# Table windows with their three parts stacked down the partitions, and a softmax table joined per block of nodes

## The chip, the cores and the metric

One core of a Trainium2 chip runs the whole kernel in one launch. The metric is the device time of one execution in microseconds. The engines are TensorE (PE, with its weight loads PEld), VectorE (DVE), ScalarE (ACT), GpSimd (POOL) and SyncE (SP). DMAs are issued from SP, ACT and, for the indirect ones, POOL.

## The reference

A graph of N = 6250 nodes with F = 128 features and E = 100000 edges. Edges come sorted by their destination `dst`; the sources `src` are random. `x` goes through two layers, each added to its input and normalised:

```python
# layer 0: attention over the edges, 8 heads of 16
q, k, v = (x @ W.T + b).reshape(N, 8, 16)           # for Wq, Wk, Wv
scores = sum(q[src] * k[dst], -1) / 4 + edge_attr_8
ex = exp(scores - segment_max(scores, src)[src])
weights = ex / segment_sum(ex, src)[src]             # softmax over a source's edges
out = segment_sum(v[src] * weights, dst) @ Wo.T + bo
x = layernorm(x + out)
# layer 1: a message of each edge, summed at its source
h = silu(concat(x[src], x[dst], edge_attr_2) @ eW1 + eb1)
fe = silu(h @ eW2 + eb2)
agg = segment_sum(fe, src)
x = layernorm(x + silu(concat(x, agg) @ nW1 + nb1) @ nW2 + nb2)
```

All of it is float32.

## The kernel before, in words

The edges are padded to 784 tiles of 128, taken in 49 chunks of 16 tiles (`UC`). The first 9 chunks are the near region (destinations in the first two blocks of 128 nodes), the other 40 the far region. `REG` holds the two; `r` is 0 for near and 1 for far. A node block is 128 rows; there are 49.

**How a row of a table reaches an edge.** A table such as q is held in DRAM as three bfloat16 parts side by side, whose sum is the float32 value. Edges of a sorted run touch few nodes that lie near each other, so a *window* of 128 consecutive rows is loaded, 128 partitions of 3 x 128 values. A one-hot matrix with a column for each edge (`hot_of`, an `is_equal` of a broadcast row of offsets with the partition's number) picks each edge's row on PE, one product for each of the three parts, summed in PSUM. `regs` reads a window's first row from an index tile into a register for the DMA.

**Stages, in order.**

1. *Sort*, beside the projections to q, k, v. The edges come by `dst` and leave by `src`. A chunk's loads (`prep_loads`: L734 `lob`, L736 `drow`, L740 `sk`, L742 `ri`, L745 four windows `kw`, one per four tiles) go out on SP. `chain` (L765 to 780) walks the 16 tiles: ACT copies a running count (`cs`, L777), PE adds a tile's histogram to it (`base`, L778) and looks up each edge's place (`look`, L780). `spread_k` (L787) fetches k's rows with `ohd` (L758) and ACT copies them into the record `stg` (L789). `rank` (L762) is a DVE count. `pick` and `send` (L794 to 809) work out the positions, and 16 scatters on POOL (L126) write records of 141 floats to `xs`. Near-region scores run in between once their records are there; `near_scores` writes the near region's softmax statistics per node to the DRAM table `near_tab`.
2. *Scores and messages* of the far region, 40 chunks. The steps are laid out as a plan: each step of a chunk has a lag in chunks, the list is sorted by time and emitted in that order, with a few rules (`held`, `run`) on what must come first. `fetch` loads the sorted records and the q windows (L518), `turn` transposes the index columns and writes the edge features' rows for later, `score` is the q products (L587) times k (L590, L591), `soft` and `stat` form maximum and sum of each source inside the chunk and add them into `stat_r` (L657, L663). `merge` joins a window of `stat_r` with one of `near_tab`: it loads `z` (L942) and the v windows `vw` (L945), copies the window of `stat_r` (L949, `tmp`), transposes it (L954), reduces (L955), pools the parts (`pooled`), takes the reciprocal and splits the result in three (`lw`); 48 products (L968) look it up and DVE and ACT form the weight `wt`. `message` multiplies v's rows (L979) with it (L982) and POOL scatters 16 tiles to `xmsg` (L126), back in the order of `dst`. The near region's messages run in the same plan and are summed by one-hot products (L1016 to 1021).
3. *Sum by destination* (L1099 to 1112) and the *node stage* (L1124 to 1165): the residual, the norm, and two tables for the edge layer, `a` for sources (three parts) and `b` for destinations (float32).
4. *Edge MLP*, in steps of four tiles, 160 far and 36 near. `loads_of` makes the one-hots (L1184, L1188), loads the edge features' 18 rows (`eft`, L1200) and the windows of a (`aw`, L1204). `pre_of` gathers b's rows on POOL (L118, `bt`), transposes them into PSUM (L1217; near steps use products with `b_near`, L1222), adds the edge features' product (L1224, `wef`) and a's three (L1228). `second` is the second layer (L1237, L1240) and `total` sums by source (L1251 `ohf`, L1255, L1259). The node MLP of a group of blocks follows as soon as its blocks are complete (L1265 on).

Windows are taken every two tiles in the near region and every four in the far one (`WT = (2, 4)`).

Of the kernel before, what the change touches and what calls it, by code (L numbers as in the profile page):

```python
# [32 lines left out]
WT = (2, 4)  # L33
PER_BLOCK = (377.5, 1671.0)
SLACK = (512.0, 1024.0)
# [17 lines left out]
def tile_gnn(  # L53
# [28 lines left out]
    q3_tab, k3_tab, v3_tab, a3_tab = (dram.tile([NW, 3 * F], BF16, name=f"{n}3_tab") for n in "qkva")  # L82
    b_tab = dram.tile([NP, F], F32, name="b_tab")
    ka_tab = dram.tile([NW, 3 * F], BF16, name="ka_tab")
    near_tab = dram.tile([NW, 16], F32, name="near_tab")
# [52 lines left out]

    def rows_of(table, j0, n):
        return table[j0 * P:(j0 + n) * P, :].rearrange("(j p) f -> p j f", p=P)  # L140
# [11 lines left out]
    for b in range(1, AB):  # L152
# [3 lines left out]
        nc.vector.tensor_scalar_add(iota_f2[b], iota_f, float(b * P))  # L156
    cnt = const.tile([P, NB], F32, name="cnt")
    xflag = const.tile([1, 1], I32, name="xflag")
    dq = const.tile([P, TU], F32, name="dq")
    d0q = const.tile([1, 208], I32, name="d0q")  # L160
    slo = const.tile([P, TU], F32, name="slo")
    s0i = [const.tile([1, n], I32, name=f"s0i{i}") for i, n in enumerate((80, 176))]
# [18 lines left out]
    def load_keys(r):  # L181
# [13 lines left out]
        for i in range(g):  # L195
            nc.sync.dma_start(d0r[r][:, i:i + 1],
                              bass.AP(tensor=dst_r.tensor, offset=dst_r.offset + (t0 + i * p) * P,
                                      ap=[[4 * P, p // 4], [0, 4], [1, 1]]))
# [70 lines left out]
    def rows_of_keys(r):  # L269
# [8 lines left out]
        if r == 0:  # L278
            nc.gpsimd.memset(none, -1.0)
            zero = ks.tile([P, 3 * F], BF16, name="zero")  # L280
            nc.gpsimd.memset(zero, 0.0)
            for tab in (k3_tab, q3_tab, v3_tab, a3_tab):
                nc.sync.dma_start(tab[NP:NW, :], zero)
# [17 lines left out]
        if r == 0:  # L301
            nc.vector.tensor_scalar_min(d0q[:, :nt // 4], kd[r][0:1, 0:nt:4], float(AB * P - 1))
        else:
            nc.vector.tensor_copy(d0q[:, t0 // 4:(t0 + nt) // 4], kd[r][0:1, 0:nt:4])
# [8 lines left out]
        if r == 0:  # L313
            nc.vector.memset(bad, 0.0)
            nc.vector.memset(d0q[:, NQ:], 0)
        b = bad[:, 4 * r:4 * r + 4]
        over = ks.tile([p, g, P], F32, name=f"over{r}")
# [4 lines left out]
        nc.vector.tensor_single_scalar(b[:p, 1:2], b[:p, 1:2], float(P), ALU.is_ge)  # L322
# [3 lines left out]
        if r == 1:  # L326
            d0qf = ks.tile([1, nt // 4], F32, name="d0qf")
            nc.vector.tensor_copy(d0qf, d0q[:, t0 // 4:NQ])
# [4 lines left out]
                                 spread[:, :, None].to_broadcast([P, nt // 4, 4]))  # L333
            yield
# [46 lines left out]
    def counts_fit():  # L381
# [6 lines left out]
        half = kp.tile([P, 2], F32, name="half")  # L388
        nc.vector.tensor_single_scalar(half[:, 1:2], iota_p, float(P // 2), ALU.is_ge)
        nc.vector.tensor_scalar(half[:, 0:1], half[:, 1:2], -1.0, 1.0, ALU.mult, ALU.add)  # L390
        sums = bank()[:, :NB]
        nc.tensor.matmul(sums[:2, :], half, cnts[1], start=True, stop=True)
        nc.vector.tensor_reduce(b[:2, 2:3], sums[:2, :], AX.X, ALU.min)
        nc.vector.tensor_single_scalar(b[:2, 2:3], b[:2, 2:3], float(4 * P), ALU.is_lt)
# [17 lines left out]
    def project_qv():  # L412
# [8 lines left out]
        nc.scalar.mul(bqv[:, 0], bqv[:, 0], D ** -0.5)  # L421
        for j0 in range(0, NB, 2):
# [12 lines left out]
            for a in range(3):  # L435
# [5 lines left out]
                for i, tab in enumerate((q3_tab, v3_tab)):  # L441
                    nc.sync.dma_start(
                        tab[j0 * P:(j0 + n) * P, a * F:(a + 1) * F].rearrange("(j p) f -> p j f", p=P),
# [5 lines left out]
    def weights():  # L449
# [21 lines left out]
        nc.sync.dma_start(parts.rearrange("i r f -> r i f"), p3)  # L471
        for i in range(3):
            for f in range(2):
                nc.sync.dma_start(wef[6 * i + 3 * f:6 * i + 3 * f + 3, :], parts[i, f:f + 1, :].to_broadcast([3, F]))
# [4 lines left out]

    def scorer(r, sp, bank_q, bank_x, deep, dsti=None):  # L480

        c0, n = REG[r]
        nw = UC // WT[r]
        works = {}
        s0b = sp.tile([P, n * nw], F32, name="s0b", bufs=1)
        minus = sp.tile([P, 1], F32, name="minus", bufs=1)
        equal = [sp.tile([P, P + 1], BF16, name=f"equal{i}", bufs=1) for i in range(3)]
        v96 = [sp.tile([P, UC, 96], BF16, name=f"v96_{i}", bufs=1) for i in range(2)]
        diag8 = sp.tile([P, UC], BF16, name="diag8", bufs=1)

        def begin():
# [3 lines left out]
                                           ap=[[XW, 1], [WT[r] * P * XW, n * nw], [1, 1]]))  # L495
# [6 lines left out]
            nc.vector.memset(s0i[r][:, n * nw:], 0)  # L502
# [1478 lines left out]
```

## Time and profile before

| | us |
|---|---|
| median of 3 runs | 4228.26 (4224.49 to 4229.2) |
| profiled execution | 4211.11 |
| its span | 4209.2 |

| engine | busy us | share of the span |
|---|---|---|
| PE (matmul) | 2643.5 | 63% |
| PEld (weight load) | 2030.1 | 48% |
| POOL | 2156.6 | 51% |
| DVE | 1994.6 | 47% |
| ACT | 861.8 | 20% |

The mean granted TensorE clock was 0.713. In a profile, a group's row gives the line of the kernel, the engine, the operation with output and inputs by the program's names, and how often it ran; then the busy time and the mean of one in ns; then how long the engine had been idle just before, and what ended most of that. "issue" means that nothing in the profile held it. A matmul's duration is from its issue to its end, and matmuls overlap; a matmul group's mean is therefore longer than what one more product costs.

### The profile page before, as it was taken

The numbers are of one execution on the slowest core, as the hardware profiler recorded it, in microseconds if no ns is written. First come the engines' busy times: TensorE is split into PE (matmuls) and PEld (weight loads), VectorE is DVE, ScalarE is ACT, GpSimd is POOL, SyncE is SP. The second block draws the span as 40 slices with busy tenths as digits, with TensorE's granted clock in tenths as the row PEclk, the third lists the DMA queues.
The fourth block names the chain that finished last, engine by engine and source line by source line (L and its number), as shares of the span: only waits on it lengthen the run. The fifth ranks groups of instructions, "written<-read, shape, count | busy, mean of one in ns | idle before, by whom it ended". The sixth has DMA issues, their size and how long they took to land. (4 is left out here: it accounts for less than half of the span.)

```text
span 4209.2 us, 65902 instructions
## 1 busy us (share of the span) xinstructions
PE 2643.5 (63%) x22552; PEld 2030.1 (48%) x22552; DVE 1994.6 (47%) x6056; ACT 861.8 (20%) x2688; POOL 2156.6 (51%) x2119
## 2 busy tenths in 40 slices
PE   6546674444444225555655666565895999898988
PEld 4444443333333224444544555454883666665655
DVE  6655335454545525555555556554892222222232
ACT  2222232122222111111111111110022222222222
POOL 3455544555555551445445444556216666666663
PEclk8555555566555556666676777576897899999999
DMA  5433545444543315434434344431754333333341
GB/s 180 130 118 103 143 138 168 139 151 132 167 130 100 110 60 142 135 109 133 122 113 127 114 120 117 138 98 50 281 197 128 109 100 98 99 110 98 101 124 46
DMA packets 492378, 523.75 MB, mean 124 GB/s; under 512 B 155562, under 2 KB 417117, under 8 KB 486912
## 3 DMA queue, kind: packets, MB, share of 16 engines
q1 hardware_dynamic: 399150, 345.09, 28.3%
q0 software_dynamic: 66048, 140.62, 10.9%
q10 hardware_dynamic: 26834, 33.73, 2.5%
q8 instruction: 180, 2.95, 0.3%
q14 instruction: 166, 1.36, 0.1%
HBM read 391.11 MB, written 128.06 MB: 123 GB/s over the span
## 5 line engine op out<-in xcount | busy, mean ns | idle before, releaser
L126 POOL DMA_INDIRECT xs<-stg,posi x784 | 803.9, 1025 | 766.1 <-ACT cs L777 337.0
L126 POOL DMA_INDIRECT xmsg<-msg,at x640 | 648.7, 1014 | 722.1 <-issue 409.4
L118 POOL DMA_INDIRECT bt<-b_tab,dsti x640 | 640.5, 1001 | 333.4 <-issue 165.4
L778 PE MATMUL base<-hi,lo 128*128 128x49 bf16 x784 | 169.6, 216 | 547.3 <-ACT cs L777 333.5
L780 PEld LDWEIGHTS <-hit 128*128 128x128 bf16 x2352 | 145.7, 116 | 546.5 <-issue 531.0
L1259 DVE TENSOR_TENSOR stat_r<-stat_r,ps 128x128 f32 x232 | 66.3, 286 | 645.7 <-PE ps L1255 223.4
L787 PE MATMUL kx<-kw,ohd 128*128 128x128 bf16 x2352 | 265.5, 284 | 97.0 <-issue 56.9
L762 DVE TENSOR_SCALAR_CACHE_REDUCE junk<-sk,meta 128x127 bf16<-128x127 int16 x784 | 298.1, 435 | 11.4 <-DMA sk<-skew 4.8
L777 ACT CAST cs<-base 128x49 bf16<-128x49 f32 x784 | 160.7, 205 | 638.3 <-remote 286.4
L787 PEld LDWEIGHTS <-ohd 128*128 128x128 bf16 x2352 | 213.9, 131 | 136.1 <-issue 129.3
L587 PEld LDWEIGHTS <-oht 128*128 128x128 bf16 x2352 | 219.3, 134 | 124.3 <-issue 63.8
L1255 PE MATMUL ps<-ohf,fe 128*128 128x128 f32 x1568 | 231.4, 292 | 52.1 <-issue 28.5
L587 PE MATMUL qv<-qw,oht 128*128 128x128 bf16 x1920 | 200.5, 287 | 97.7 <-DVE oht L576 36.3
L1240 PE MATMUL po<-w_sb,ht 128*128 128x128 f32 x1568 | 245.6, 301 | 18.7 <-issue 9.4
L1255 PEld LDWEIGHTS ps<-ohf,fe 128*128 128x128 f32 x1568 | 208.8, 205 | 62.0 <-issue 33.9
L1240 PEld LDWEIGHTS po<-w_sb,ht 128*128 128x128 f32 x1568 | 205.2, 203 | 66.8 <-issue 49.4
L979 PE MATMUL qv<-vw,oht 128*128 128x128 bf16 x1920 | 188.5, 257 | 74.2 <-DVE pr L590 34.0
L1232 ACT ACTIVATE ht<-pre 128x512 f32<-128x512 f32 x196 | 116.9, 597 | 493.1 <-PE pre L1228 199.6
L979 PEld LDWEIGHTS <-oht 128*128 128x128 bf16 x1920 | 152.9, 117 | 122.6 <-issue 92.3
L223 DVE TENSOR_TENSOR lo<-iota_e,lo_c 128x2048 bf16<-128x2048 bf16 x98 | 119.0, 1215 | 150.6 <-remote 80.2
L780 PE MATMUL look<-st_b,hit 128*128 128x49 bf16 x1568 | 164.3, 211 | 27.1 <-DVE sel L794 17.0
L1228 PE MATMUL pre<-oht,aw 128*128 128x512 bf16 (+1 forms) x696 | 171.9, 365 | 12.8 <-issue 12.4
(303 smaller groups left out, 5228.8 us busy)
## 6 DMA issues: line engine op xcount, KB each, us to landing
st<-xs SPq DMA_DIRECT2D x49, 1128.0 KB
srow<-slo_row SPq DMA_DIRECT2D x98, 512.0 KB
lob<-lob_row SPq DMA_DIRECT2D x49, 512.0 KB
drow<-dlo_row SPq DMA_DIRECT2D x49, 512.0 KB
sk<-skew SPq DMA_DIRECT2D x49, 508.0 KB
qw<-q_tab SPq DMA_DIRECT2D x232, 96.0 KB
vw<-v_tab SPq DMA_DIRECT2D x232, 96.0 KB
aw<-a_tab SPq DMA_DIRECT2D x232, 96.0 KB
```

Source lines behind the costliest of these rows:

```text
L118: nc.gpsimd.indirect_dma_start(out=dst, out_offset=None, in_=table, in_offset=bass.IndirectOffsetOnAxis(ap=idx, axis=0))
L126: apart(nc.gpsimd.indirect_dma_start(out=table, out_offset=bass.IndirectOffsetOnAxis(ap=idx, axis=0), in_=src, in_offset=None), group)
L587: nc.tensor.matmul(qe[:, i, :], w["oh"][:, 4 * q + i, :], w["qw"][:, (4 * q + i) // WT[r], k, :], start=(k == 0), stop=(k == 2))
L762: nc.vector.tensor_scalar(junk, w["sk"][:, :, j], meta[:, c * UC + j, 0:1], 0.0, ALU.is_equal, ALU.add, accum_out=w["rank"][:, j:j + 1])
L777: nc.scalar.copy(cs, base)
L778: nc.tensor.matmul(base, lo, hi, start=False, stop=False, skip_group_check=True)
L780: nc.tensor.matmul(w["look"][:, j - 8 * h, :], w["hit"][:, j, :], tab, start=(i == 0), stop=(i == 2))
L787: nc.tensor.matmul(kx[:, i, :], w["ohd"][:, 4 * q + i, :], w["kw"][:, q, a, :], start=(a == 0), stop=(a == 2))
L979: nc.tensor.matmul(ve[:, i, :], w["oh"][:, 4 * q + i, :], w["vw"][:, (4 * q + i) // WT[r], k, :], start=(k == 0), stop=(k == 2))
L1228: nc.tensor.matmul(pre[:, i * wt:(i + 1) * wt, :], w["aw"][:, 4 // wt * q + i, k, :], w["oh"][:, 4 * q + i * wt:4 * q + (i + 1) * wt, :], ...
L1240: nc.tensor.matmul(po[:, i, :], ht[:, i, :], cw["w2"], start=False, stop=(i == 3))
L1255: nc.tensor.matmul(ps[:, i // WT[r], :], fe_[:, i, :], oh[:, i, :], start=(i % WT[r] == 0), stop=((i + 1) % WT[r] == 0))
```

## The change

1. *Stacked windows.* The far region's windows of q, v and a, and k's windows in the sort, become short: 32 rows (`KS`) or 42 (`KD`) per two tiles, with the three parts below each other on 96 or 126 partitions. The one-hot gets three copies of the offset pattern down the partitions, so one product sums the three parts. A window per two tiles means eight loads a chunk instead of four. The near region keeps its 128-row windows and three products.
2. *Softmax table per node block.* `merge` goes. A new step `settle`, 49 times, takes one block of `stat_r` when its statistics are complete, joins it with the near statistics (kept in SBUF, so `near_tab` goes), and writes the three parts into 16 columns more of v's table, which becomes 144 wide (`VW`). Each v window then brings the table with it; `load` and `weigh` are the steps that read it. The lags of the plan are raised.
3. *Edge features below a's rows.* In far steps of the edge MLP the 18 rows of the edge features lie on partitions 96 to 113 under the one-hot, and their weights under a's window, so one product of 114 rows does both; `wef`'s own product goes.
4. The one-hots for the sums by source (`soh`, `ohf`) and their results have 72 columns instead of 128 in the far region, and the conditions for taking this path are adapted to the shorter windows.

```diff
+KD = 42
+KS = 32
+WA = (2, 4)
+WN = (P, 72)
+VW = F + 16
+    def stacked(table, row, n, width):
+        return table[bass.ds(row, n), :].rearrange("n (i f) -> i n f", f=width)
...
-        kw = bw.tile([P, 4, 3, F], BF16, name="kw")
-        for q in range(4):
-            nc.sync.dma_start(kw[:, q].rearrange("p i f -> p (i f)"),
-                              (k3_tab if r else ka_tab)[bass.ds(kreg[c // 4][4 * (c % 4) + q], P), :])
+        kw = bw.tile([3 * KD, 8, F], BF16, name="kw")
+        for q in range(8):
+            nc.sync.dma_start(kw[:, q], stacked(k3_tab if r else ka_tab, kreg[c // 2][8 * (c % 2) + q], KD, F))
...
-            for a in range(3):
-                nc.tensor.matmul(kx[:, i, :], w["ohd"][:, 4 * q + i, :], w["kw"][:, q, a, :],
-                                 start=(a == 0), stop=(a == 2))
+            t = 4 * q + i
+            nc.tensor.matmul(kx[:, i, :], w["ohd"][:, t, :], w["kw"][:, t // 2, :], start=True, stop=True)
...
+        none = pj.tile([P, 1, VW - F], BF16, name="nostat", bufs=1)
+        nc.gpsimd.memset(none, 0.0)
+        for a in range(3):
+            nc.sync.dma_start(v3_tab[:NP, a * VW + F:(a + 1) * VW].rearrange("(j p) f -> p j f", p=P),
+                              none.to_broadcast([P, NB, VW - F]))
...
+            if r:
+                t = sp.tile([kw, nw, width], BF16, name=name, bufs=bufs)
+                for i in range(nw):
+                    nc.sync.dma_start(t[:, i], stacked(tab, rg[i], KS, width))
...
+            if r:
+                nc.tensor.matmul(to, oh[:, t, :], tab[:, t // 2, part], start=True, stop=True)
+            else:
+                for k in range(3):
+                    nc.tensor.matmul(to, oh[:, t, :], tab[:, t // 2, k, part], start=(k == 0), stop=(k == 2))
...
+            def settle(b, q):
+                x = bank_x()[:, :96]
+                nc.tensor.transpose(x, sums_of["src"][:96, b * P:(b + 1) * P], ident[:96, :96])
+                z = sp.tile([P, 1, 3, 16], F32, name="z")
+                nc.vector.tensor_reduce(z[:, 0, 0:2].rearrange("p a v -> p (a v)"),
+                                        x.rearrange("p (k v) -> p v k", v=32), AX.X, ALU.add)
+                nc.scalar.copy(z[:, 0, 2], sums_of["near"][:, b])
+                o = sp.tile([P, 1, 16], F32, name="o")
+                pooled(o, z, sp, 1, 3)
+                nc.vector.tensor_scalar_max(o[:, :, 8:16], o[:, :, 8:16], 0.5)
+                nc.vector.reciprocal(o[:, :, 8:16], o[:, :, 8:16])
+                o3 = sp.tile([P, 3, 16], BF16, name="o3")
+                split3([o3[:, k, :] for k in range(3)], o[:, 0], sp, "orest")
+                nc.scalar.dma_start(v3_tab[b * P:(b + 1) * P, :].rearrange("p (k f) -> p k f", k=3)[:, :, F:], o3)
+            def weigh(r, w, s):
+                x = bank_x()[:, :256].rearrange("p (t v) -> p t v", v=16)
+                for t in range(UC):
+                    s["looked"](x[:, t, :], w["oh"], t, w["vw"], slice(F, VW))
...
+            def far_load(c, q):
+                works[c]["vw"] = s["window"](v3_tab, c, "vw1", 3, VW)
...
-            steps = {"fetch": (s["fetch"], 1, 6.0), "turn": (s["turn"], 3, 5.0), "score": (s["score"], 4, 4.0),
-                     "soft": (s["soft"], 2, 3.0), "stat": (s["stat"], 4, 2.25), "merge": (far_merge, 4, 0.9),
-                     "message": (far_message, 4, 0.0)}
+            steps = {"fetch": (s["fetch"], 1, 8.5), "turn": (s["turn"], 3, 7.5), "score": (s["score"], 4, 6.5),
+                     "soft": (s["soft"], 2, 5.5), "stat": (s["stat"], 4, 4.75), "load": (far_load, 1, 1.5),
+                     "weigh": (far_weigh, 1, 0.7), "message": (far_message, 4, 0.0)}
...
+            kw = 3 * KS
+            aws = [el.tile([kw + 18, UC // 2, F], BF16, name=f"aw1{i}", bufs=1) for i in range(2)]
+            for aw in aws:
+                nc.scalar.dma_start(aw[kw:], cw["wef_d"][:, None, :].to_broadcast([18, UC // 2, F]))
...
-                nc.tensor.matmul(flat, cw["wef"], w["eft"][:, 4 * q * P:4 * (q + 1) * P], start=False, stop=False)
-                wt = WT[r]
-                for i in range(4 // wt):
-                    for k in range(3):
-                        nc.tensor.matmul(pre[:, i * wt:(i + 1) * wt, :], w["aw"][:, 4 // wt * q + i, k, :],
-                                         w["oh"][:, 4 * q + i * wt:4 * q + (i + 1) * wt, :],
-                                         start=False, stop=((i + 1) * wt == 4 and k == 2))
+                    nc.tensor.matmul(flat, cw["wef"], w["eft"][:, 4 * q * P:4 * (q + 1) * P], start=False, stop=False)
+                for i in range(2):
+                    oh = w["oh"][:, 4 * q + 2 * i:4 * q + 2 * i + 2, :]
+                    for k in range(1 if r else 3):
+                        nc.tensor.matmul(pre[:, 2 * i:2 * i + 2, :],
+                                         w["aw"][:, 2 * q + i, :] if r else w["aw"][:, 2 * q + i, k, :], oh,
+                                         start=False, stop=(i == 1 and k == (0 if r else 2)))
```

## The prediction

> **What bounds the kernel now.** I read the page's slices first, then busy time by stage, then the costliest groups, then the chain of the sort. Rows: engine, busy tenths in 40 slices of 105 us; PEclk is the granted clock.
>
> ```profile
> PE   6546674444444225555655666565895999898988
> DVE  6655335454545525555555556554892222222232
> POOL 3455544555555551445445444556216666666663
> PEclk8555555566555556666676777576897899999999
> ```
>
> No engine is full for long: there are three plateaus. From the first starts of the three groups of indirect DMAs on POOL they are the sort (0 to 1580 us), the score and message stage (1580 to 2955; with the sum by destination to 3183) and the edge MLP (3183 to 4209). A stretch out of the middle of each:
>
> ```profile
> core 0: us, PE busy (x) PEld busy (x) DVE busy (x) ACT busy (x) POOL busy (x), PEclk, DMA share, GB/s
> 900.00:1575.00 675.00, 262.48 (x2945) 222.98 (x2942) 324.65 (x1212) 145.70 (x579) 365.83 (x360) 0.58 0.40 120
> 1700.00:2850.00 1150.00, 675.11 (x7203) 568.46 (x7202) 642.31 (x1857) 178.93 (x717) 566.30 (x558) 0.68 0.41 119
> 3190.00:4190.00 1000.00, 882.70 (x5173) 590.50 (x5172) 258.87 (x635) 237.22 (x406) 628.84 (x628) 0.91 0.36 100
> ```
>
> PE is 39% busy in the sort, 59% in the scores, 88% in the MLP. So a removed product is worth its full time only in the last stage; in the others it is worth what it holds up. The groups:
>
> ```profile
> L126 POOL DMA_INDIRECT xs<-stg,posi x784 | 803.9, 1025 | 766.1 <-ACT cs L777 337.0
> L126 POOL DMA_INDIRECT xmsg<-msg,at x640 | 648.7, 1014 | 722.1 <-issue 409.4
> L118 POOL DMA_INDIRECT bt<-b_tab,dsti x640 | 640.5, 1001 | 333.4 <-issue 165.4
> L787 PE MATMUL kx<-kw,ohd 128*128 128x128 bf16 x2352 | 265.5, 284 | 97.0 <-issue 56.9
> L587 PE MATMUL qv<-qw,oht 128*128 128x128 bf16 x1920 | 200.5, 287 | 97.7 <-DVE oht L576 36.3
> L979 PE MATMUL qv<-vw,oht 128*128 128x128 bf16 x1920 | 188.5, 257 | 74.2 <-DVE pr L590 34.0
> L1228 PE MATMUL pre<-oht,aw 128*128 128x512 bf16 (+1 forms) x696 | 171.9, 365 | 12.8 <-issue 12.4
> ```
>
> The second number after the bar is one instruction's latency; back-to-back matmuls overlap, so I cost products by start-to-start time in the trace. POOL's indirect DMAs cannot follow each other closer than 1.25 to 1.27 us (median start-to-start): a floor of 20.3 us for each chunk of 16. The shape of a product matters little but for its columns:
>
> ```profile
> L1224 PE MATMUL pre<-eft,wef 18*128 18x512 bf16 x196 | 78.9, 403 | 3.1 <-issue 3.1
> L1222 PE MATMUL pre<-ohd,b_near 128*128 128x512 bf16 x216 | 58.0, 408 | 0.2 <-issue 0.2
> ```
>
> 18 rows take 403 ns, 128 rows 408: rows stacked down the partitions come free.
>
> **Sort, costed: -70 us (0 to -170).** kx (L787) goes from 2352 to 784 products. Four follow each other in 0.60 us and twelve in 0.85 (the timeline below and its neighbours), so about 100 ns each and 157 us of PE for the 1568 removed. The stage is not held by PE, though:
>
> ```profile
> 1483.36 0.60 PE L787 MATMUL kx<-kw,ohd 128*128 128x128 bf16 x4
> 1485.26 0.96 POOL L126 DMA_INDIRECT xs<-stg,posi  x1 [9.18 <-ACT cs L777]
> 1495.25 6.28 SPq L745 DMA_DIRECT2D kw<-k_tab  x4
> ```
>
> Where nothing else is going on (1423 to 1540 us) a chunk takes 29.1 us: 16 scatters at 1.26 = 20.2, then a 9 us hole, in which ACT's cs and PE's base hand a running count to and fro every 0.5 us, then DVE picks positions. Some 24 kx stand in that hole: four of them stretch a link from 0.50 to 0.59 us, eleven run just ahead of the first copy. With a third of them left, three links save 0.09 us each and the run 0.75: 1 us a chunk, 49 chunks, -50. In the 33 us chunks that share PE with near-region work more of the 3.2 us of kx per chunk is on the path, so up to -110 without stretching it; I take -70. Loads: eight windows of 32 KB for four of 96 KB. SP took 1.57 us for each kw load in the row above, so 6.3 us more per chunk; SP is at most 36% busy here (10.5 us of 29), so a chunk's loads, which are issued for the next one, stay hidden. Without that cover: 49 x 6.3 = +308.
>
> **Scores and messages, costed: -250 us (-80 to -330).** Start-to-start, L587's products take 104 ns, L979's 103, L968's 42. Each drops from 1920 to 640 in the far region: 1280 x 249 ns = -319. The transposes of L954 go from 232 to 49 (187 ns): -34. The sums L657 have 72 columns for 128 (123 ns): about -27. Together -380 of PE, or 9.5 us in each of 40 chunks that now take 32.5 us (scatters 1649.5 to 2950.5). In the stretch above PE has 777 us start-to-start and 370 us of waits; if those stayed, a chunk would be 23.0 us. But DVE (642 of 1150, so 18.2 us a chunk) loses only small things (232 tmp copies at 231 ns, part of the 1216 ns soh), and POOL needs 20.3; with three engines that near to each other the waits grow. I take 25.5 us, between 23.0 and 32.5 and nearer the first since the lags of the plan are also longer: -7 x 40 = -280. Longer lags (fetch 8.5 chunks ahead, for 6) make the ramp longer, about one chunk more: +25 to +30. -250. SP has 417 of 1150 us issuing; eight more window issues a chunk at 0.58 us, less four z reads at 0.42: about 14 us of 25, not a bound.
>
> **A wait that is new: the settle.** 49 times ACT issues the write of a node block's softmax columns into v3_tab; this write waits until window loads of the same table have landed, and later loads wait for the write. Behind it on ACT stand the cs, exp and v casts. No row of before shows it. The plan puts 0.5 chunk (12 us) on both sides of it, so the value is 0; the other end is 10 us (in the trace some seven for a window load from issue to landing and three for a small write) x 49 = +490. I stay near 0 because ACT is 16% busy in this stage, and keep a part for the range. Below nothing it cannot go; the merge's own DVE work is in the sum already.
>
> **Rule against row: the engines of a stacked window.** The page moves 345.09 MB on q1 in 28.3% of 16 engines:
>
> ```profile
> q1 hardware_dynamic: 399150, 345.09, 28.3%
> ```
>
> that is 0.283 x 16 x 4209 us / 399150 = 47.7 ns a packet on average, 865 bytes each. The Trainium skill, "DMA: Bandwidth & Descriptors", section on why a DMA increments its semaphore by 16, says that a load runs on the largest number of engines up to 16 that divides both slowest dimensions. A stacked window has 3 parts outermost: 3 engines, where a 128-row window has 16. The score stage then puts 16 windows x 32 = 512 rows of 256 to 288 bytes per chunk on each of three engines. At the row's 47.7 ns that is 24 us, plus some 10 us of other traffic: 34 us, no gain at all there (sum -195). Packets of 256 bytes, the nearest in size, last 19.4 ns on average in the trace: 10 us, beside 10 of other traffic, in 25.5. I follow the packets of that size. Spread over 16 engines it would be 2 us and free.
>
> **Edge MLP, costed: -125 us (-80 to -165).** A far step loses the 512-column wef product (344 ns start-to-start) and three 512-column ones (270 ns), 1.15 us, and gets two of 256 columns (150 ns): -0.85 x 160 = -137. L1255 gets 72 columns, but its weight loads at 133 ns each stand; -15. PE's 912 us (start-to-start) become 760, with the stretch's 88 us of waits 848. POOL's 640 gathers at 1.25 to 1.30 us need 800 to 833 us, so it nearly meets a floor: I take 885 for 1010, -125. The eight 24 KB loads per chunk (for four of 96) go ahead into two buffers, and SP issues for only 236 of 1026 us in this stage: 0; uncovered, four more at 0.58 us in 40 chunks are +93.
>
> **The clock, rule against row.** PEclk is 0.58, 0.68 and 0.91 at PE shares of 39, 59 and 88%. The skill's "TensorE: Matmul & The Clock Gate", Part 1, says that the array falls to half clock after an idle window of some 3.4 us. A leaner PE leaves more holes. By the row, the scores' 104 ns products are near half pace already, so nothing is lost; the MLP at 75% share may fall from 0.91 to about 0.84: 8% of 760 = +60. By the rule taken to the end (half clock) its products would be 1.8 times longer and the stage no shorter. I keep the row, and the +60 in the range.
>
> **Nothing:** three zero fills of v3_tab lie in the early stage beside the sort; 0. near_tab's 12 writes and 232 8 KB reads go from queues that held no one; 0. Settle's one transpose, reduce and pooling per block replace as many per chunk; inside the 25.5.
>
> **Sum.** -70 - 250 - 125 = -445 against the profiled 4211.1 us (span 4209.2), 3766; the median of the runs is 17 us above the profiled one, so 4228.3 - 445 = 3783 us.
>
> **Rivals.**
> - *The score stage keeps its pace.* For: its waits are spread over DVE, ACT and DMA, and three engines carry every window. Against: the largest waits before L587 and L979 are for DVE's oht and pr, whose PSUM banks come free sooner. Then 0 to -80 there: total -150 to -275, 3950 to 4075.
> - *More than the sum.* The hand-over in the sort goes faster without kx, POOL's idle time put down to cs (337 us in L126's row) shrinks by half, and the scores reach 23 us: -600 to -700, about 3580.
> - *Slower.* The settle blocks ACT until windows on three crowded engines land: at 10 us x 49 it costs 490 and exceeds the sum; with sort and MLP unchanged from my sum, 445 is met at 9.1 us a settle. At 11: about 4320.
> - *The short path is not taken*, if a pair of tiles spans over 42 or 32 rows. With these inputs the widest are 34 and 23; I give it no chance.
>
> **Chances.** Forecast 0.55, scores unchanged 0.20, more than the sum 0.12, slower 0.12, no change 0.01. The 0.2% that a measurement can tell from nothing is 8 us, far from most cases. The range leaves out half of the two outer cases: 3560 to 4030.
>
> **What would show it.** The profile after should have kx x784, L587's and L979's heirs at 640 far products, PE below 45% in the scores and near 75 to 80% in the MLP with POOL above 70%. Right: xmsg scatters 25 us a chunk apart. Wrong: POOL's hole before xmsg put down to a DMA of vw or qw or to ACT behind the settle; vw's median time to landing above 10 us; the sort still at 29 us a chunk with kx gone. A clock under 0.8 in the MLP would make the rule right.

## The result: 5.1% slower, and the profile after

The changed kernel takes 4442.8 us (median of 4 runs, 4434.5 to 4473.7) against 4228.7 for the kernel before: ratio 1.051, 95% interval 1.045 to 1.057. The forecast was 3783 us. Its profiled span is 4442.7 us, 233.5 more than before. The slices of its page:

```profile
PE   5435663332333213344334334432975878788877
POOL 3445445454453551344454445466026566655552
PEclk7555555555555555555555555555996888877878
```

PE is emptier all the way, as meant, and so is everything else: no engine took over. A stretch out of each stage (sort, scores, MLP), to be read against those of before:

```profile
core 0: us, PE busy (x) PEld busy (x) DVE busy (x) ACT busy (x) POOL busy (x), PEclk, DMA share, GB/s
900.00:1640.00 740.00, 228.12 (x2348) 171.13 (x2346) 344.84 (x1288) 155.09 (x609) 363.03 (x367) 0.52 0.39 114
1800.00:3040.00 1240.00, 498.25 (x3979) 365.36 (x3978) 553.02 (x1748) 174.74 (x764) 593.58 (x591) 0.56 0.34 97
3410.00:4330.00 920.00, 752.75 (x4256) 574.70 (x4255) 186.41 (x560) 205.09 (x355) 543.46 (x555) 0.79 0.32 85
```

PE's share went from 39, 59 and 88% to 31, 40 and 82%, the granted clock from 0.58, 0.68 and 0.91 to 0.52, 0.56 and 0.79. The groups that belong to those shown of before:

```profile
L132 POOL DMA_INDIRECT xs<-stg,posi x784 | 794.2, 1013 | 859.2 <-issue 381.0
L132 POOL DMA_INDIRECT xmsg<-msg,at x640 | 636.9, 995 | 785.4 <-issue 244.4
L124 POOL DMA_INDIRECT bt<-b_tab,dsti x640 | 626.8, 979 | 427.3 <-issue 166.8
L849 PE MATMUL kx<-kw,ohd 126*128 126x128 bf16 x784 | 135.2, 297 | 54.9 <-issue 46.7
L1311 PE MATMUL po<-w_sb,ht 128*128 128x128 f32 x1568 | 280.7, 328 | 46.5 <-issue 24.8
```

The products are gone as written (kx x784), but POOL sits idle for longer in front of all three of its groups (766, 722 and 333 us before), and a product that nobody touched, L1311 (L1240 before: 301 ns), has become 9% longer. With POOL's first and last start of each group as marks, the stages of all profiled runs on this chip are (us):

| | sort's last scatter | then to first message | messages | to first gather | gathers | rest |
|---|---|---|---|---|---|---|
| before | 1574.5 | 75.0 | 1301.0 | 223.6 | 973.6 | 61.5 |
| the change | 1658.0 | 103.7 | 1324.1 | 244.4 | 1053.0 | 59.5 |
| e1, rows interleaved | 1624.5 | 93.0 | 1224.8 | 242.1 | 994.7 | 50.2 |
| e2, MLP's reads as before | 1658.9 | 103.0 | 1332.4 | 244.9 | 1006.5 | 59.1 |
| e3, sort's reads as before | 1615.6 | 102.9 | 1332.6 | 242.2 | 1059.5 | 54.3 |
| e4, fillers in the MLP | 1639.6 | 103.4 | 1329.6 | 242.4 | 1105.9 | 56.9 |

The stages are those of the profiled execution, which in e2 and e3 was 28 and 20 us longer than the median of that kernel's runs.

The loss lies in the sort (+84), the fill before the first message (+29), the messages (+23), the stretch up to the first gather (+21) and the MLP (+79).

### The profile page after: what moved, and what is told of

Its sections match the earlier page's. It is cut to its first block, busy times and chain, and to the rows that moved or that the text cites. A ratio compares the mean times of both kernels' runs of the same rounds, so it can differ in the third digit from the quotient of the medians.

```text
span 4442.7 us, 55221 instructions
## 1 busy us (share of the span) xinstructions
PE 2284.4 (51%) x16642; PEld 1705.0 (38%) x16642; DVE 1827.0 (41%) x5869; ACT 859.4 (19%) x2737; POOL 2122.6 (48%) x2120
## 5 line engine op out<-in xcount | busy, mean ns | idle before, releaser
L132 POOL DMA_INDIRECT xmsg<-msg,at x640 | 636.9, 995 | 785.4 <-issue 244.4
L1330 DVE TENSOR_TENSOR stat_r<-stat_r,ps 128x72 f32 (+1 forms) x232 | 57.1, 246 | 765.3 <-remote 257.2
L1326 PE MATMUL ps<-ohf,fe 128*128 128x72 f32 (+1 forms) x1568 | 263.1, 323 | 116.5 <-ACT fe L1313 94.5
L824 DVE TENSOR_SCALAR_CACHE_REDUCE junk<-sk,meta 128x127 bf16<-128x127 int16 x784 | 299.4, 438 | 53.1 <-remote 21.8
L539 PEld LDWEIGHTS <-oht 96*128 96x128 bf16 x1920 | 171.8, 128 | 353.8 <-issue 250.9
L1311 PE MATMUL po<-w_sb,ht 128*128 128x128 f32 x1568 | 280.7, 328 | 46.5 <-issue 24.8
L1326 PEld LDWEIGHTS ps<-ohf,fe 128*128 128x128 f32 x1568 | 249.9, 241 | 125.1 <-ACT fe L1313 100.6
L1311 PEld LDWEIGHTS po<-w_sb,ht 128*128 128x128 f32 x1568 | 236.7, 227 | 119.1 <-issue 89.7
L1313 ACT ACTIVATE fe<-po 128x512 f32<-128x512 f32 x196 | 117.0, 597 | 381.0 <-remote 164.6
L1169 PE MATMUL ps<-ohd,mt 128*128 128x128 f32 x1280 | 152.3, 282 | 70.3 <-DMA mt<-xmsg 55.6
L855 DVE TENSOR_TENSOR sel<-look,hi 128x392 f32<-128x392 f32 x98 | 54.9, 561 | 316.6 <-PE look L842 258.6
L1169 PEld LDWEIGHTS ps<-ohd,mt 128*128 128x128 f32 x1280 | 148.9, 197 | 73.8 <-issue 54.4
L849 PE MATMUL kx<-kw,ohd 126*128 126x128 bf16 x784 | 135.2, 297 | 54.9 <-issue 46.7
L842 PE MATMUL look<-cs,hit 128*128 128x49 bf16 x784 | 157.8, 219 | 2.5 <-issue 2.5
```

Source lines behind the costliest of these rows:

```text
L132: apart(nc.gpsimd.indirect_dma_start(out=table, out_offset=bass.IndirectOffsetOnAxis(ap=idx, axis=0), in_=src, in_offset=None), group)
L539: nc.tensor.matmul(to, oh[:, t, :], tab[:, t // 2, part], start=True, stop=True)
L824: nc.vector.tensor_scalar(junk, w["sk"][:, :, j], meta[:, c * UC + j, 0:1], 0.0, ALU.is_equal, ALU.add, accum_out=w["rank"][:, j:j + 1])
L842: nc.tensor.matmul(w["look"][:, j - 8 * h, :], w["hit"][:, j, :], tab, start=(i == 0), stop=(i == 2))
L849: nc.tensor.matmul(kx[:, i, :], w["ohd"][:, t, :], w["kw"][:, t // 2, :], start=True, stop=True)
L1169: nc.tensor.matmul(ps, mt[:, 4 * q + i, :], oh[:, i, :], start=(i == 0), stop=(i == 3))
```

## What the trace after shows first: SP's issue

Instructions of SP that load the q windows, before:

```profile
L512 SPq DMA_DIRECT2D qw<-q_tab x232: 3/333/3563, 658.2 to 2744.9; - x116
```

and after:

```profile
L529 SPq DMA_DIRECT2D qw<-q_tab x320: 3/738/2393, 1667.4 to 2840.1; - x160
L533 SPq DMA_DIRECT2D qw<-q_tab x72: 3/333/2620, 689.4 to 1346.1; - x72
```

The three figures are the shortest, median and longest issue in ns. L529 is the stacked window, three blocks of 32 rows; L533 is the near region's window of 128 rows, whose form did not change. A stacked window costs SP 738 ns where a plain one costs 333, and there are twice as many. Its packets also overlap in the trace mostly one to four at a time (over 90% of the time in which any is under way in the messages) where those of a 128-row window spread evenly over one to sixteen: that agrees with the three engines that the rule of the Trainium skill ("DMA: Bandwidth & Descriptors", section on why a DMA increments its semaphore by 16) gives for it. Who waits for loads on SP, and for one scatter, stands in the list of waits (engine, line, releaser: us in total, times, longest):

```profile
DVE oht L549 <- DMA srow<-slo_row: 151.5, 17, 30.6
ACT at L645 <- DMA xmsg<-msg,at: 84.4, 14, 10.9
PE x L539 <- DMA vw<-v_tab: 82.0, 70, 7.8
```

The first is DVE at a one-hot, up to 31 us at a time, for a row of offsets that SP loads (35.6 us in 10 waits before). The second is a wait that no step of the prediction had: ACT at turn. The third is PE at the softmax table, for a window of v.

## Experiments on the chip of the result

Two theories stood against each other. W: the stacked windows' loads are the cost, through SP's queue and the three engines. C: a leaner PE gets a lower clock, and what is left of its work takes longer.

**e1: the same windows as consecutive lines.**

```diff
-        return table[bass.ds(row, n), :].rearrange("n (i f) -> i n f", f=width)
+        return table[bass.ds(row, n), :].rearrange("n (i f) -> (n i) f", f=width)
...
+    nc.vector.tensor_scalar(iota_s, iota_p, 1.0 / 3.0, -1.0 / 3.0, ALU.mult, ALU.add)
+    nc.vector.tensor_copy(third, iota_s)
+    nc.vector.tensor_copy(iota_s, third)
```

`third` is an int32 tile, so the copy rounds to a whole number.

> The changed kernel, with the three parts of a row next to each other on the partitions (row 0 part 0, 1, 2, row 1 ...), so that a window is 96 or 126 consecutive lines of 256 bytes instead of three blocks; the one-hot's pattern is the partition's number divided by three. Same products, same bytes. Theory W (the stacked window's DMA is the cost: 0.74 us of SP for each issue where a 128-row window takes 0.33, and three DMA engines): issue falls to about 0.35 us, the packets spread over many engines, SP's busy time in the score stage falls from 685 to about 450 of 1190 us, and the time falls from 4443 to 4250 or less. Theory C (PE does less, its granted clock falls to 0.55 in scores and 0.79 in the MLP, and every product is longer): no more than 30 us of it come back, 4410 to 4445.

Measured: 4229.2 us, ratio to before 1.001 (0.999 to 1.003). SP's issue of the far windows of q:

```profile
L528 SPq DMA_DIRECT2D qw<-q_tab x320: 1/317/3050, 1633.5 to 2697.9; - x160
```

317 ns, below that of a 128-row window, and the packets overlap up to ten at a time. One line of address order takes back 214 us, as much as the change had lost: 34 in the sort, 11 in the fill, 99 in the messages, 58 in the MLP. That is theory W, for 214 us. But these are not the same losses stage by stage: against before, e1 still stands at +50 in the sort, +18 in the fill, +19 up to the first gather and +21 in the MLP, and at -76 in the messages. Nor does it say where the 445 us went that the change should have gained, since e1 has every removed product removed and stands level with before. Of the three waits only the last went down with the dear loads:

```profile
DVE oht L548 <- DMA srow<-slo_row: 135.2, 12, 31.0
ACT at L644 <- DMA xmsg<-msg,at: 119.0, 21, 13.3
PE x L538 <- DMA vw<-v_tab: 32.8, 18, 6.6
```

**e2: MLP's far reads as before.** `pre_of` and `loads_of` get back four windows of 128 rows and three products of 512 columns, beside `wef`.

> The changed kernel, with only the far reads of the edge MLP as before the change: four windows of 128 rows a chunk, three products and the edge features' own product (the rows picked are then not those of the offsets, which changes the values and not the work). Sums by source stay at 72 columns. Theory C: the granted clock in the MLP goes back to about 0.91 and the stage from 1053 us of gathers to about 975: total near 4365. Theory W: the same gain from the windows, but e1 shows it too. If neither: the stage stays at 1050 and the total at 4440.

Measured: 4379.0 us, ratio 1.036 (1.032 to 1.039). Its MLP:

```profile
3420.00:4300.00 880.00, 792.15 (x4545) 525.86 (x4543) 188.36 (x565) 205.35 (x353) 538.03 (x556) 0.89 0.35 101
```

The gathers take 1006 us, 47 less than with the lean MLP of the change (the medians of the runs are 64 apart), though PE has more to do, by the prediction's count 137 us. The clock is 0.89. e1's MLP, with the lean products and cheap loads, takes 995. So with the loads paid for alike, leaving out four of the far products gains nothing to speak of.

**e3: the sort's k windows as before.** `kw`, `drow` and `ohd` on 128 partitions, four loads, three products (windows at every second of the two-tile offsets, so the rows picked differ and the work does not).

> The changed kernel, with only the sort's k windows as before: four windows of 128 rows a chunk and three products. If the eight stacked loads on SP delay lob, drow and sk behind them (theory W), the last scatter of the sort comes back from 1658 us to about 1575 and the total to about 4360. If the clock is what counts in the sort (theory C), about the same with PEclk near 0.58 instead of 0.53. If the sort's loss is from something else in the change (near-region steps that run in between), it stays at 1640 to 1670.

Measured: 4389.0 us, ratio 1.038 (1.034 to 1.042). The sort's last scatter comes at 1616 us for 1658, half of the way back to 1575. The same wait of DVE in this run:

```profile
DVE oht L549 <- DMA srow<-slo_row: 54.0, 17, 6.3
```

54 us for 151.5, and none over 6.3. But e1 has this wait too (135.2 us), with issues of 317 ns, so it is not the price of a stacked load. Where near-region steps run in between, from the first scatter of chunk 24 to that of chunk 40, the sort takes 490 us before, 563 in the change, 554 in e1 and 504 in e3: some 74 of the 84 us lie here, and the address order gives back 9 of them. In this stretch the change and e1 each have three chunks of 46 to 51 us, and in each a wait of DVE for `srow` of 28 to 31 us. SP's own list of waits for the change (849 to 1413 us of its trace) and for e1 (825 to 1379) says where SP stood:

```profile
SPq L533 <- DMA slo_row<-sr: 56.4, 4, 27.3
SPq L533 <- DMA dst_row<-db: 35.5, 2, 20.7
SPq L532 <- DMA dst_row<-db: 99.4, 3, 49.8
SPq L532 <- DMA slo_row<-sr: 51.5, 4, 24.7
```

It stands in front of a near-region q window, whose form did not change, until a row that ACT writes has landed, and everything behind it on the queue waits along, `srow` first. The traces of before and of e3 have no such wait at a q window. So this part goes with eight kw loads for four, or with the leaner PE (e3 also brings back the three products, and the sort's clock from 0.53 to 0.59), and not with what a load costs; why the window waits for that write was not tested.

**e4: fillers of 18 rows in the MLP.**

```diff
+                    for k in range(2):
+                        nc.tensor.matmul(flat, cw["wef"], w["oh"][:18, 4 * q:4 * q + 4, :].rearrange("p t e -> p (t e)"),
+                                         start=True, stop=True, skip_group_check=True)
```

> The changed kernel with two added products of 512 columns at the start of each far step of the edge MLP, into the bank that the step fills next, whose result is overwritten: more work and no new wait. Theory C: the clock there rises from 0.79 to about 0.9 and the stage gets shorter, 1053 us of gathers to about 1000, total 4390 to 4410. Against C: each adds about 0.27 us to 160 steps, 85 us in all, and the total goes to 4480 to 4530, or stays where PE is not the bound.

Measured: 4491.8 us, ratio 1.064 (1.060 to 1.068); the stage took 1106 us, 53 more.

```profile
3390.00:4370.00 980.00, 852.14 (x4558) 588.54 (x4558) 188.88 (x565) 206.72 (x355) 545.86 (x561) 0.80 0.29 80
```

PE is 87% busy and the clock stays at 0.80, where the MLP of before got 0.91 at 88%. Busy time alone does not bring the clock; a product of 18 rows did not. Theory C as I had put it fell in this run.

## The same kernels on other chips

The later runs are from other chips, on which the kernel before takes 3241 us and not 4228. Times across chips can't be compared, ratios can. e9 to e12 shared one chip, e5 to e8 another, e13 to e16 a third; on these three the kernel before took 3240.5 to 3241.8.

> The kernel before, unchanged, profiled beside the next three on one chip. The second set of runs was on a chip on which the kernel before takes 3240 us and not 4227. If this is again such a chip: POOL's scatters follow at 1.26 us nearly without holes, the sort ends near 1175 to 1200 us, the MLP's gathers take about 820 (their floor), and PE, DVE and ACT all stand still for far less than the 208 us of 1150 in the score stage. If it is like the first: 4210 to 4240 and the stages of before.

> The changed kernel, unchanged, on the same chip as the next two. Theory W (stacked windows cost SP 0.74 us each and run on three engines): slower than before by 2 to 6% here as well, with an SP issue of 0.74 us; on a chip without the long stalls most of it in the score stage. If the loss of 5% belonged to the first chip's stalls alone: within 1.5% of before here.

> The interleaved kernel (e1) on the same chip. By e7, which is e1 with fillers in the MLP: score stage 960 to 980 us of scatters if this is the second chip or one like it, ratio to before 1.02 to 1.03; on one like the first 1.00.

> The interleaved kernel with twelve at buffers (e5) on the same chip as e1. Theory B (ACT waits at turn for the scatter of eight chunks before): 90 to 110 us less than e11 in the score stage, ratio to before 0.99; on a chip like the first, 60 to 110 us less than e11, ratio 0.975 to 0.985.

| | ratio to before (95%) | sort | to first message | messages | to first gather | gathers |
|---|---|---|---|---|---|---|
| e9, before | 1.001 (1.000 to 1.003) | 1156.5 | 71.7 | 939.9 | 222.8 | 818.1 |
| e10, the change | 1.045 (1.043 to 1.047) | 1174.7 | 101.1 | 1023.6 | 242.6 | 816.7 |
| e11, interleaved | 1.025 (1.024 to 1.027) | 1172.6 | 89.4 | 973.0 | 241.3 | 818.0 |
| e12, and 12 `at` buffers | 0.996 (0.994 to 0.997) | 1173.6 | 88.4 | 873.2 | 244.4 | 816.4 |

Here too the change loses 4.5%: 18 us in the sort, 29 in the fill, 84 in the messages, 20 up to the first gather. The address order is worth 64 us here, 2%, and not 214. And the gathers tell where the MLP's gain went: 640 at a start-to-start of 1.25 to 1.27 us are 800 to 813 us, and with or without the change they take 817. POOL sets the MLP on this chip; PE is 97% busy in e9 and 91% in e10, and it makes no difference. The sort is near the same bound: 784 gaps of 1.263 us are 990 us of its 1157.

**The wait for eight chunks before.** `at`, the row numbers of a chunk's scatter, has eight buffers. Turn now runs 7.5 chunks ahead of the messages, so ACT's copy into a buffer waits for scatters issued moments ago to land. In e11:

```profile
ACT at L644 <- DMA xmsg<-msg,at: 206.6, 32, 16.0
```

> The interleaved kernel (e1), with twelve instead of eight buffers for the scatter's row numbers (at). With the lags raised to 7.5 chunks, ACT's copy into that tile at turn waits for the scatter of eight chunks before: 117 us in 20 waits of up to 13 us in e1's score stage, none before the change. Theory B (this wait holds ACT, and with it the chain of exp and casts): the wait is gone, the score stage's scatters take 1225 - 60 to - 110 us, total 4120 to 4170. If the wait only stands where ACT would have stood anyway: less than 25 us, total 4205 to 4230.

```diff
-                    w["at"] = sp.tile([P, UC], I32, name="at", bufs=8)
+                    w["at"] = sp.tile([P, UC], I32, name="at", bufs=12)
```

Measured for e5: 3219.5 us, ratio 0.993 (0.991 to 0.996), messages 872 us where e7, with eight buffers on that chip, took 977. In e12 the wait has left ACT, and DVE's wait for a message buffer has grown, from 47.8 us in e11 to

```profile
DVE msg L1027 <- DMA xmsg<-msg,at: 97.1, 28, 6.8
```

100 us of messages gone for four buffers of 64 bytes a partition: 21.8 us a chunk, where POOL's floor is 20.3. On the chip of the result e1 has this wait for 119 us in 21 times; what twelve buffers give there wasn't tried.

**e6: is it the settle?**

```diff
-                nc.scalar.dma_start(v3_tab[b * P:(b + 1) * P, :] ...[:, :, F:], o3)
+                nc.scalar.dma_start(v4_tab[b * P:(b + 1) * P, :] ...[:, :, F:], o3)
```

> The interleaved kernel (e1), with settle's write going to a table of its own that no window reads, so that neither waits for the other (the weights are then not those of the softmax; the work is the same). The slower rival of the prediction (each of 49 settles holds ACT for up to 10 us): 100 us or more faster, near 4120. The prediction's value of 0 for this wait: within 20 us of e1, 4210 to 4240.

Measured: 3305.4 us, ratio 1.020 (1.017 to 1.022). Against e7 on the same chip, which has e1's score stage, the messages take 963 for 977 us: 14 us for 49 settles, 0.3 us each. The handshake that my slower rival rested on costs nearly nothing here; with the change's own loads, and on the chip of the result, it was not taken apart.

**e7: fillers of 114 rows.** As e4, on e1, with `b_near`'s rows as weights and the whole one-hot.

> The interleaved kernel (e1), with two added products of 114 rows and 512 columns at the start of each far step of the MLP, overwritten afterwards. The fillers of 18 rows left the granted clock at 0.80 with PE 87% busy. If the grant counts rows that work and not only time: the clock rises to 0.88 or more and the stage stays within 30 us of e1's 995. If the clock has another cause: it stays at 0.80 to 0.83 and the stage takes about 55 to 85 us more, total 4280 to 4315.

Measured: 3325.1 us, ratio 1.027 (1.024 to 1.030), gathers 816 us. With POOL as the bound the two fillers cost nothing. The clock of its MLP

```profile
2530.00:3270.00 740.00, 697.87 (x4689) 522.38 (x4720) 198.37 (x588) 221.59 (x368) 563.21 (x581) 0.97 0.38 109
```

is 0.97 with PE 94% busy; e5's on the same chip, without fillers, is 0.92 at 90%, and e9's 1.00 at 97%. So here the clock rose with the added products, where e4's of 18 rows left it at 0.80. That it is the rows and not the chip or the loads, no pair of runs on one chip shows; and that such fillers would shorten the stage on the first chip wasn't tried.

**e8: of the change only the score stage.** e5 with the reads of sort and MLP as before and sums of 128 columns again (values differ as in e2 and e3).

> The interleaved kernel with twelve at buffers, the sort's k windows and the MLP's far reads as before the change, and the MLP's sums at 128 columns again (four-tile windows with two-tile offsets, which changes values and not work). So of the change only the score stage stays. If the score stage is the only part that gains: sort ends near 1600, scores take 1130 to 1225, the MLP 975, total 4080 to 4190. If the parts of the sort and the MLP gained too: above e5.

Measured: 3232.0 us, ratio 0.997 (0.995 to 0.998), 13 us above e5 on the same chip: sort 1178 for 1171, gathers 822 for 819. With POOL as the bound the reads of sort and MLP are worth nearly nothing either way.

**e15: SP's issue without the three engines.**

```diff
                     nc.sync.dma_start(t[:, i], stacked(tab, rg[i], KS, width))
+                more = sp.tile([1, nw, 64], BF16, name=name + "m", bufs=bufs)
+                for i in range(nw):
+                    nc.sync.dma_start(more[:, i], tab[bass.ds(rg[i], 1), :64])
```

> The interleaved kernel with eight at buffers (e1), where each stacked window of the score stage is followed by one more load on SP, of a single row of 128 bytes into a tile that nothing reads: SP's issue time per window then is about 0.65 us, near the 0.74 of the changed kernel, while the window's own data go over many engines. If SP's issue is the cost: the score stage goes from e1's length to the changed kernel's (on a chip without the long stalls from 973 to about 1020 us). If the three engines are: within 15 us of e1's.

Measured: 3500.7 us, ratio 1.079 (1.075 to 1.082); messages 1138 us, 165 more than e11's 973 for 640 more issues of 0.23 us. DVE's wait for srow in this run:

```profile
DVE oht L551 <- DMA srow<-slo_row: 247.9, 34, 10.1
```

Neither expectation held. The added issues are some 146 us of SP's time and cost 165; the change's dear windows (e10) are 250 us more of SP's time than e11's and cost 51. So SP's busy time alone does not set the price. SP's waits in e15 and in e11, during the messages:

```profile
SPq L528 <- DMA slo_row<-sr: 95.7, 20, 7.5
SPq L528 <- DMA slo_row<-sr: 23.6, 8, 6.2
```

With the added loads SP stands four times as long in front of its windows until ACT's write has landed. So e15 shows that the stage hangs on SP's queue. It doesn't separate issue from engines, since the added loads also change what SP waits for; how the change's 51 us on this kind of chip divide between the two stays open.

**e13, e14, e16: the fill and the zero fill.** e13 is e5 with lags of 7.25, 6.5, 5.9 and 5.3 for 8.5, 7.5, 6.5 and 5.5. e14 is e5 with the zero fills of v's table on ACT's queue. e16 is both.

> The interleaved kernel with twelve at buffers (e5), lags of fetch, turn, score, soft down from 8.5, 7.5, 6.5, 5.5 to 7.25, 6.5, 5.9, 5.3 chunks. If the lags cost the fill between the last scatter of the sort and the first of the messages (88 us against 72 before): 8 to 15 us less there, and the same less in total. If the room is needed: the score stage gets longer by more than that.

> e5 with the three zero fills of the v table (37632 pieces of 32 bytes) issued on ACT's queue instead of SP's. If they hold the sort's loads that queue behind them: the sort's last scatter comes 10 to 20 us earlier, total the same less. If ACT's own issue of them holds the chain, or the sort's loss is elsewhere: no gain.

> e13 and e14 together. If each does what it is meant to: 20 to 35 us less than e5, ratio to before 0.985 to 0.99; the fastest of all here.

Measured: e13 3210.6 us, ratio 0.989 (0.985 to 0.992); e14 3226.0, 0.995 (0.993 to 0.996); e16 3216.4, 0.992 (0.989 to 0.995). e13 has its first message 83.8 us after the sort's last scatter, e14 89.8: the lags cost some 6 us of fill, and the messages take 864 against 870. The zero fill's queue makes no difference. Why the sort ends 17 us later than before on these chips stays open; it is lost in chunks 12 to 17 (131 us before, 158 and 157 in e10 and e11, 140 in e8 with four windows), and the chunks after these are, in sum, quicker than before. e13 is the fastest of all and beats both kernels, on such a chip, by 1.1% and about 5%.

**The 20 us from the last message to the first gather.** They are the same on all chips, and most of them lie in the sum by destination: its last product ends 165 us after the last scatter before, and 182 us after it in the change (165 and 182 in e9 and e12 too). In this sum DVE loads the first rows of the windows into registers. Before, they lie next to each other (`d0q`); the change keeps one for every two tiles and reads every second (`d0p[:, ::2]`):

```profile
L135 DVEq TENSOR_LOAD <-d0q x11: 846/1099/1101, 2959.1 to 3112.6; - x11
L141 DVEq TENSOR_LOAD <-d0p x11: 2744/3606/3626, 3088.9 to 3264.7; - x11
```

3.6 us for 16 numbers in place of 1.1: 27 us in all, on the engine that builds the one-hots and adds the sums. PE then waits 14.6 us for these one-hots, 1.7 before. SP shows the same price: 3.4 us in e3, whose k windows take every second offset, and 1.2 us in the change, which loads 16 neighbours. A run with the numbers packed again was not made.

## Why the prediction was wrong, step by step

- *What bounds the kernel* was read rightly in one half: PE is not full in sort and scores. The other half failed: I took PE's removed time as gain wherever waits "stayed". In the scores PE lost 319 + 34 us and more, and e1's messages shrank by 76, e11's grew by 33, and e12's, with neither dear loads nor the wait for `at`, shrank by 67.
- *Sort, -70.* The chunks with nothing beside them did fall, from 29.1 to 28.2 us, near the 1 us worked out. The failed term is "a chunk's loads stay hidden". I priced an issue by rows of the old form (the row's 6.28 us for four loads is its whole length, with gaps; one issue had a median of 338 ns), counted SP's busy time, and not who stands behind a load that waits: `srow`, and DVE for it. Measured: +84, of which the address order gives back 34 (e1) and the old windows 42 (e3); the rest is open.
- *Scores, -250.* The lag term met the number (fill +29 against +25 to +30), in part by luck: 11 of it are the loads (e1), and half of the added lag gave back 6 (e13). The messages came out at +23 for -280. Two terms failed. That SP is "not a bound" is one: the loads cost 99 us on the first chip (e1) and 51 on the other kind (e11). The other: I asked of the longer lags only what they add to the ramp, not which buffers they outlive. Eight `at` buffers at a lag of 7.5 cost 100 to 106 us on the other chips (e12 against e11, e5 against e7). On the first chip what is missing beyond the 99 us was not taken apart: the wait for `at` is there, and PE, DVE and ACT are at rest together for longer (last section). The forecast of 25.5 us a chunk against a floor of 20.3 was in reach without that and the dear loads: e12 runs at 21.8, e11 at 24.3, the change at 25.6 on those chips; but there the kernel before already runs at 23.5, where on the first it took 32.5 and the change 33.1.
- *Rule against row, the engines of a window.* The rule (three engines) is what the trace shows, and the packets' 18 to 21 ns were sized well. Neither had the 738 ns of SP for each issue; which of the two, issue or engines, made the loss stays open (e15).
- *The settle, 0.* Right, as far as measured: 0.3 us each (e6). The slower rival had the sign of the result and the wrong mechanism.
- *MLP, -125, and the clock.* Measured on the first chip: +79. The first failed term is again the loads, taken as 0: 58 us (e1). The second is the gain itself. I kept the row against the rule and put the +60 in the range. The clock was 0.79 and, without the dear loads, 0.82, and the stage still 21 us longer than before (e1). L1310's mean is 321 ns there where L1240's was 301. The criterion that the text gave for the rule ("under 0.8") was met. The waits grew as well: all of PE, DVE and ACT at rest for over 1 us fills 107 us of 960 in e1 and 60 of 1000 before. How much is clock and how much hand-over stays open. On the other chips POOL's floor hides it all: this was named as the bound that PE "nearly meets", and was the bound.
- *Nothing* for the rest: false by 21 us between the last message and the first gather. The register loads of every second number were no term of the sum.
- *A sum of the rivals.* With -70 and -125 from my own sum, "scores unchanged" gives -195 to -275 and not -150 to -275; it changes nothing in the outcome.

## What to carry to other kernels

A DMA's address order is a cost of its own: the same bytes as three blocks or as consecutive lines differed by 0.42 us per issue on an in-order queue, and by 5% of the kernel on one chip, 2% on another. A queue that works in order also passes on the waits of each entry: look for who stands behind a load that waits. When lags in a software pipeline are raised, go through every tile that lives across the lag and compare its buffers with it. Before counting removed products as time, find the engine that paces the stage when nothing waits: here, on three chips of four, indirect DMAs on POOL at 1.25 to 1.27 us. Numbers that are loaded into registers should lie next to each other: 16 of them took 1.1 us so, 3.6 us at a stride of two.

## What the runs showed of the hardware

The largest effect in this study is the chip: the same kernel takes 4228 us on one and 3241 on three others. On the first there are stretches in which POOL issues indirect DMAs and the other engines nearly stand. From the kernel after:

```profile
1485.09 12.31 SPq L808 DMA_DIRECT2D kw<-k_tab  x6
1498.81 0.69 SPq L797 DMA_DIRECT2D lob<-lob_row  x1
1501.61 0.69 SPq L799 DMA_DIRECT2D drow<-dlo_row  x1
1504.41 0.69 SPq L803 DMA_DIRECT2D sk<-skew  x1
1506.51 0.96 POOL L132 DMA_INDIRECT xs<-stg,posi  x1 [0.30 <-issue]
1507.20 0.70 SPq L805 DMA_DIRECT2D ri<-rec_in  x1
1508.65 0.20 ACT L839 CAST cs<-base 128x49 bf16<-128x49 f32 x1 [22.46 <-issue]
```

(start, duration, instruction, and in brackets the idle time before it). SP moves by one load each 2.8 us, ACT stands for 22.5 us and goes on 1.2 us after POOL's last scatter has ended. In the score stage all of PE, DVE and ACT are at rest for over 1 us at a time for 209 of 1150 us before and 350 of 1190 after; on the chip of e9, 32 of 840. A DMA issue is no dearer there (median 738 ns for the change's q windows, 742 in e10), but SP's register instructions before it are: in the messages they take 0.14 us on average and up to 1.4 in the change, 0.04 and under 0.05 in e10. Whether POOL's issuing holds the others, and why this chip alone does so, was not found. There the same address order costs 214 us, and 64 on e10's chip.
